# New load order, placement and rank tables in a gated cross-attention and expert kernel

## The chip, the cores and the metric

The kernel runs on one core of a Trainium2 chip. Its time is the device time of one execution in microseconds (us); the median of three runs is compared. TensorE is called PE in the profile, VectorE DVE, ScalarE ACT, GpSimd POOL and SyncE SP.

## The reference

Two token blocks of 1024 rows of 2048 values (x) and two contexts of 2048 by 2048 (ctx) give two gated steps:

```
q1 = fake_quant(layernorm(x), s1, z1)      # round, clip to 0..255, back
q2 = fake_quant(ctx, s2, z2)
x  = x + tanh(g_xattn) * (q1 @ q2)
n  = layernorm(x)
logits = n @ route_w.T                     # 8 experts, the best one is taken
h  = n @ A.T                               # 8 experts x 16
x  = x + tanh(g_ffn) * (onehot(best) * best_logit * h) @ Bw
```

## The kernel before

The 2 x 1024 rows are 16 tiles of 128 rows (eight for each batch); the 2048 output columns are four strips of 512. A tile and a strip make a group: 16 products of 128x128 by 128x512 in float16 (line 718), added up in one PSUM bank. VectorE then adds the result to the tile of x (739, or 747 and 752).

Before that, a tile needs its statistics (bn_stats on VectorE, line 573, for tiles in `STATV`; else a sum and a sum of squares on ScalarE, 591 and 601), an inverse root on GpSimd (623), small scale values on VectorE (613 to 619), quantisation on ScalarE (637), a clamp on VectorE (643), and turning: by eight PE transposes twice (674) and two copies out of PSUM (535, called from 681; the second on VectorE for tiles in `COPYV`), or by one DMA transpose for tiles in `TURN` (664). For tiles in `SPLIT`, VectorE quantises the second half (646, 652). A row sum corrects for the zero points (689 on VectorE for tiles in `SUMV`, 691 on ScalarE).

A context strip comes in four chunks of 1 MB (443), or in two halves each for chunks in `FINE`. A chunk is quantised on ScalarE (450) and clamped on VectorE (457), or, for chunk halves numbered 2 x chunk + half in `VQ`, both on VectorE (461, 468). Its column sums come from 16 PE products with ones (493) for strips in `ONES`, else from VectorE additions and one product (504 to 519).

After a tile's four groups follows the second step: the tile is turned (by PE, 836, and ScalarE copies, 850; or, for tiles in `MOVE`, by VectorE block transposes, 774, and DMA moves, 792, which go by way of DRAM for tiles in `VIA`, 784 and 797, and are issued half on ScalarE's queue for tiles in `TWO`), multiplied with the weights (842 or 818), routed on VectorE (910 to 919), turned back (932, 938), multiplied again (945), added (953) and stored (966 on GpSimd's queue, 959 for the last tile). Tiles in `LATE` add the correction beforehand (730).

All instructions are tasks of a plan. A task has an engine, a cost, a rank, the tasks that it needs and the buffers that it takes. `walk` goes through a model of the engines and, on each engine that is free, picks the ready task of lowest rank that has room; the order found is the order of the program, and on the chip each engine keeps to it. `XL0` and `XLEAD` set the ranks of the loads of x, `CTX` and `CQ` those of context chunks, `LEAD` those of a tile's preparation, `SUM` of its row sum, `COR` of a strip's column sums, `AFTER` and `POR` of the second step and of its output products. `PIECES` cuts a load of x, `XPOOL` puts it on GpSimd's queue; tile 0's second and fourth pieces go by ScalarE's. `SLACK` is added in the model to the landing of loads of x. `XL` loads wait for the last context chunk. At most eight transfers are under way on SyncE's and ScalarE's queues together, and eight on GpSimd's. A DMA transpose is started only when the model's DMA is idle.

The groups run in sets, each set going strip by strip through its tiles:

```
sets = [[0, 1, 2], [3], [4], [5, 6, 7], [8, 9]] + [[t] for t in range(10, NT)]
```

A group's rank is its number in this order, so tiles 0, 1 and 2 share the first strips. The first instructions on PE are warm-up products on a constant (367).

Of the kernel before, what the change touches and what calls it, by code (L numbers as in the profile page):

```python
# [42 lines left out]
class Plan:  # L43
# [11 lines left out]
    def add(self, eng, cost, rank, fn, needs=(), bufs=(), nbytes=0, alone=False, slack=0.0, parts=1):  # L55


        t = Task()
        t.eng, t.cost, t.rank, t.fn, t.nbytes = eng, cost, rank, fn, nbytes
        t.alone, t.slack, t.parts = alone, slack, parts  # L60
        t.needs, t.bufs, t.start, t.end = list(needs), list(bufs), None, None
        for b in bufs:
            b.left += 1
        self.tasks.append(t)
        return t
# [99 lines left out]
def flamingo_gated_kernel(  # L165
# [40 lines left out]
    BLK = 32  # L206


    TURN = {4, 6, 11, 12, 13, 14, 15}
    MOVE = {3, 4, 6, 8, 10, 11, 12, 13, 14}  # L210
    pools = {"big": 10, "q2": 4, "half": 3, "q1t": 5, "wh": 2, "wht": 2, "bn": 3, "sel": 2, "away": 2}
    kinds = {k: (k, n) for k, n in pools.items()}
# [13 lines left out]
    def buf(kind, name, shape, dt):  # L226
        pool = kinds[kind][0]
        where = {"bank": psum, "away": away}.get(pool, work)
        return Buf(kind, lambda u: where.tile(shape, dt, tag=f"{pool}{u}", name=name))
# [68 lines left out]
                whole[t, s] = i  # L298


    LATE = {4, 5, 6, 7, 10, 15}
    STATV = {0, 1, 3, 5, 12, 13, 14}
    SUMV = {2, 5, 6, 8, 12, 14}
    COPYV = {0, 3, 4, 5, 7, 9, 14}
    ONES = {0}
    SUM = [0.5, 8.5, 2.5, 1.5, -1, 1.5, 1.5, 2.5, 5.5, 2.5, 8.5, 1.5, 8.5, 8.5, 1.5, 8.5]
    LEAD = [6, 14, 10, 8, 6, 5, 8, 14, 5, 5, 8, 14, 4, 6, 4, 6]
    XLEAD = [4, 4, 4, 4, 0, 4, 3, 10, 2, 10, 3, 1, 4, 2, 6, 0]
    XL0 = {0: -101, 1: 2.2, 2: -4.0, 3: 4.4}
    AFTER = [1.2, 6.2, 2.2, 2.2, 0.3, -0.8, 4.2, 5.2, -0.8, 3.2, 6.2, 6.2, 4.2, 1.7, 5.2, 2.2]  # L310
    CTX = [8, 6, 5, 5, 5, 5, 4, 3]
    COR = [2.5, 1.5, 7.5, 0.5, 1.5, 1.5, -0.5, 0.5]
    SLACK = 4.0
    VIA = {0, 2, 3, 5, 9, 12, 14}
    TWO = {0, 1, 4, 5, 7, 9, 11, 13, 15}
    XL = {15}
    PIECES = {0: 4, 1: 4, 2: 2, 3: 4}
    SPLIT = {0}
    FINE = {3, 6}
    VQ = {0, 4, 5, 6, 8, 9, 15, 17, 19, 21, 27, 33, 39, 44, 51}  # L320
    XPOOL = {2}
    POR = [0, 0, 1.5, 1, 0, 2, 1.5, 0, 1.5, 0.5, 0, 0.5, 0, 1, 2, 1.5]
    BN2 = set()
    CQ = {4: -1.2, 5: -1.6, 0: 1.2, 11: -1.3, 9: -0.9, 3: 0.6, 7: 0.8, 8: -0.9, 2: 1.3, 6: -2.0, 10: -1.1, 1: 1.3}
    SP, ACT, DVE, PE, POOL = "SP", "ACT", "DVE", "PE", "POOL"
    add = plan.add

# [98 lines left out]
    def strip(b, s):  # L426
# [5 lines left out]
        for q in range(NQ):  # L432
            st = flat(f"st{b}", f"st_{b}_{s}_{q}", F32, D)
            key = (b * NN + s) * NQ + q
            H = 2 if key in FINE else 1
            n = QK // H
            for h in range(H):
                rank = i - CTX[b * NN + s] + (q + h / H) * len(tiles) / NQ + CQ.get(key, 0)
                k = q * QK + h * n
# [31 lines left out]

                on_v = 2 * key + h in VQ
                a = t_ctx[b, s, q] = add(
# [11 lines left out]
        cs = buf("cs", f"cs_{b}_{s}", [P, NC], F32)  # L485
        rank = i + COR[b * NN + s]
        if b * NN + s in ONES:
# [46 lines left out]
    def copy(on_vector, o, i):  # L534
        (nc.vector.tensor_copy if on_vector else nc.scalar.copy)(o, i)  # L535

    def tokens(t):

        b, m = divmod(t, MT)
        early = t == 0  # L540
        rank = first[t] - LEAD[t]
        xb[t] = xx = buf("xl" if t in XL else "x", f"x_{t}", [P, D], F32)
        pieces = PIECES.get(t, 1)
        w = D // pieces
        loads = []
        for i in range(pieces):
            queue = (
                (ACT, nc.scalar) if early and i % 2 else (POOL, nc.gpsimd) if t in XPOOL else (SP, nc.sync)
            )
            loads.append(  # L550
                add(
                    queue[0], 0.5, XL0.get(t, rank - XLEAD[t]),
                    lambda i=i, queue=queue: queue[1].dma_start(
                        xx.ap()[:, ts(i, w)], x[b, ts(m, P), ts(i, w)]
                    ),
                    [t_ctx[1, NN - 1, NQ - 1]] if t in XL else [t_ctx[0, NN - 1, 1]] if t > 3 else [], [xx], nbytes=4 * P * w, slack=SLACK if t > 3 else 0.0 if t else 1.0,
                )
# [9 lines left out]
        mean, var, nmean, ssum = (mv[:, i : i + 1] for i in range(4))  # L567
        if t in STATV:
            bn = buf("bn", f"bn_{t}", [P, NN, 6], F32)
# [41 lines left out]
        def scale():  # L611
# [5 lines left out]
            nc.vector.scalar_tensor_tensor(nb, nmean, a, z1, ALU.mult, ALU.add)  # L617
            if t in SPLIT:
                nc.vector.scalar_tensor_tensor(nv, nmean, a, zm1, ALU.mult, ALU.add)
# [4 lines left out]
        )  # L624
        ts_ = add(DVE, 1.0 if t in SPLIT else 0.8, rank, scale, [pw, t_rs, t_nm])
        if t == 0:
            t_sc.needs.append(ts_)
        q1t[t] = qt = buf("q1t", f"q1t_{t}", [P, KC, P], F16)
        H = 2 if early or t in SPLIT else 1
        hw = D // H  # L630
# [3 lines left out]
        for h in range(H):  # L634
# [18 lines left out]

            on_v = h == 1 and t in SPLIT
            d = add(
# [4 lines left out]
            t_read.setdefault(t, []).append(d)  # L660
        if t in TURN:
            a_ = add(
# [5 lines left out]
            t_turned.append(a_)  # L668
        for h in range(0 if t in TURN else KC // 8):
            pt = buf("tp", f"pq_{t}_{h}", [P, 8, P], F16)  # L670

            def turn(h=h, pt=pt):
                for j in range(8):
# [5 lines left out]
                add(  # L679
                    DVE if h and t in COPYV else ACT, 0.7 if h and t in COPYV else 1.0, rank,  # L680
                    lambda h=h, pt=pt: copy(h and t in COPYV, qt.ap()[:, ts(h, 8), :], pt.ap()),
                    [a_], [pt, qt],
# [3 lines left out]
        def row_sum():  # L686
            p = qb.ap()
            if t in SUMV:
                nc.vector.tensor_scalar(p, p, 0.0, 0.0, ALU.add, ALU.add, accum_out=rw)
# [3 lines left out]
        d = add(  # L693
            DVE if t in SUMV else ACT, 2.3 if t in SUMV else 2.1, first[t] + SUM[t], row_sum, clamps + t_turned, [qb]
        )
        t_r[t] = add(
            DVE, 0.25, first[t] + SUM[t],
            lambda: nc.vector.tensor_scalar(r, rw, cd2, ckd, ALU.mult, ALU.add), [d, t_sc],  # L698
# [7 lines left out]

    late = LATE

# [53 lines left out]
    def hidden_moved(t, xx, hl, rank):  # L762
# [17 lines left out]
        moved = []  # L780
        if t in VIA:
            there = buf("away", f"away_{t}", [P, D], F32)
# [4 lines left out]
        for g in range(BPC):  # L787
            on, queue = (ACT, nc.scalar) if t in TWO and g % 2 else (SP, nc.sync)

# [6 lines left out]
            def fetch(g=g, queue=queue):  # L796
# [6 lines left out]
                add(on, 0.55, rank - 0.5, fetch, [w], [there, across], nbytes=4 * P * NC)  # L803
                if t in VIA
                else add(on, 2.4, rank - 0.5, move, turns, [turned, across], nbytes=4 * P * NC, parts=4)
# [50 lines left out]
    def ffn(t):  # L856
        b, m = divmod(t, MT)
        end = t == NT - 1
        rank = last[t] + AFTER[t]
        xx = xb[t]  # L860
# [65 lines left out]
        a = add(DVE, 1.5, rank - 1, route, [p, t_r2, t_set], [hl, wh, sel_b])  # L926
        behind = rank + POR[t]
        pw = buf("tp", f"pw_{t}", [P, NC], F32)
# [96 lines left out]
```

## Time and profile before

| what | us |
|---|---|
| median of 3 runs | 392.39 (392.09 to 394.58) |
| profiled execution | 393.32 |
| its span | 391.4 |
| TensorE busy | 375.3 |
| VectorE busy | 307.8 |
| ScalarE busy | 228.6 |
| main products, 1024 of line 718, share of the chain of work | 56% |
| output products, 128 of line 945, share of the chain | 14% |

The span is what the trace covers of the profiled execution. The chain of work follows the end of the program back, at each step to what released it, so its shares say which engine the time was spent on. Pipelined products overlap in the busy time: a main product is listed with 379 ns, while they follow each other every 0.216 us. Slices are fortieths of the span. The mean granted clock of TensorE is 0.993.

### The profile page before, as it was taken

The page shows a single profiled execution, that of the slowest core. Times are in us where ns is not written, and L with a number is a line of the kernel's source. Part 1 is how long each engine was busy: PE and PEld are TensorE (multiplying, and loading weights), DVE is VectorE, ACT ScalarE, POOL GpSimd, SP SyncE. Part 2 cuts the span into 40 slices and gives each one's busy share as a digit, 9 for nine tenths or more (in the row PEclk, how much of TensorE's full clock was granted, in tenths as well). Part 3 has the DMA queues.
Part 4 walks back from the last instruction along what each step waited for, and adds up shares of the span by engine and source line. Part 5 has one row for each costly group of instructions (what it writes and reads, how often), then busy time and mean ns, then how long its engine had stood idle before and what let it go on. Part 6 is the DMA issues. An engine that isn't in the chain of part 4 may idle for free.

```text
span 391.4 us, 5431 instructions
## 1 busy us (share of the span) xinstructions
PE 375.3 (96%) x2001; PEld 219.0 (56%) x2001; DVE 307.8 (79%) x709; ACT 228.6 (58%) x219; POOL 22.9 (6%) x54
## 2 busy tenths in 40 slices
PE   5689999999999999999999999999999999999993
PEld 5544545667754464644565754656444664664671
DVE  4599999997786869789888898978989698575243
ACT  1689995489903553887989897556225620430420
POOL 4000000001001000001000010000110000001000
PEclk9899999999999999999999999999999999999998
DMA  7999999601357926989388986348364466509305
GB/s 246 394 386 387 386 351 415 234 0 37 126 215 296 249 60 204 327 316 379 98 207 293 391 353 185 122 137 262 154 127 108 91 225 175 190 42 266 125 1 214
DMA packets 47043, 85.88 MB, mean 219 GB/s; under 512 B 17704, under 2 KB 19752, under 8 KB 43048
## 3 DMA queue, kind: packets, MB, share of 16 engines
q1 hardware_dynamic: 43060, 66.66, 52.3%
q0 software_dynamic: 2512, 16.78, 10.9%
q10 hardware_dynamic: 1444, 2.10, 2.1%
q8 instruction: 15, 0.25, 0.3%
q14 instruction: 12, 0.10, 0.1%
HBM read 55.64 MB, written 19.92 MB: 193 GB/s over the span
## 4 chain that ended last, share of the span: by engine, by line
PE 91%; ACT 3%; DMA 2%; issue 1%; POOL 1%; DVE 0%; POOLq 0%; ACTq 0%
PE mm L718 56%; PE po L945 14%; PE hl L818 9%; PE hl L842 7%; PE px L836 3%; DMA x<-in_x_dram 2%; PE pq L674 2%; ACT q L637 1%; ACT q L450 1%; ACT q L601 1%; ACT q1t L535 1%; ACT q L691 0%; PE pw L932 0%; PE cs L519 0%; POOL row L265 0%
## 5 line engine op out<-in xcount | busy, mean ns | idle before, releaser
L718 PE MATMUL mm<-q,q1t 128*128 128x512 f16 x1024 | 233.3, 379 | 0.7 <-ACT q1t L535 0.7
L718 PEld LDWEIGHTS <-q1t 128*128 128x128 f16 x1024 | 99.8, 98 | 119.1 <-issue 10.9
L450 ACT ACTIVATE q<-st,raw,rs 128x2048 int16<-128x2048 f32 (+1 forms) x29 | 57.6, 2003 | 11.7 <-PE mm L718 8.7
L945 PE MATMUL po<-wb,wht 128*128 128x512 f32 x128 | 60.6, 595 | 0.4 <-ACT wht L938 0.4
L953 DVE SCALAR_TENSOR_TENSOR x<-po,th,x 128x512 f32<-128x512 f32 x64 | 47.1, 748 | 13.2 <-PE po L945 10.7
L637 ACT ACTIVATE q<-x,mine 128x2048 int16<-128x2048 f32 (+1 forms) x16 | 32.6, 2040 | 24.2 <-DVE mine L617 14.8
L899 ACT ACTIVATE junk<-x,mine 128x2048 f16<-128x2048 f32 x16 | 32.1, 2007 | 15.4 <-DVE mine L698 8.0
L818 PEld LDWEIGHTS hl<-war,turned 128*128 128x128 f32 x288 | 34.8, 190 | 2.7 <-issue 1.1
L818 PE MATMUL hl<-war,turned 128*128 128x136 f32 x288 | 35.3, 280 | 0.1
L945 PEld LDWEIGHTS po<-wb,wht 128*128 128x128 f32 x128 | 23.4, 190 | 21.3 <-issue 14.9
L747 DVE SCALAR_TENSOR_TENSOR x<-mm,sc,x 128x512 f32<-128x512 f32 x40 | 29.4, 744 | 4.1 <-PE mm L718 3.7
L752 DVE SCALAR_TENSOR_TENSOR x<-x,mine,corr 128x512 f32<-128x512 f32 x40 | 29.4, 746 | 1.1 <-DVE x L747 0.5
L814 ACT COPY turned<-across 128x1024 f32<-128x1024 f32 x18 | 18.0, 1040 | 20.2 <-DMA across<-away 15.0
L842 PE MATMUL hl<-war,xt 128*128 128x136 f32 x224 | 28.9, 279 | 0.0
L842 PEld LDWEIGHTS hl<-war,xt 128*128 128x128 f32 x224 | 27.9, 190 | 1.6 <-issue 0.5
L739 DVE SCALAR_TENSOR_TENSOR x<-mm,sc,x 128x512 f32<-128x512 f32 x24 | 17.6, 746 | 12.4 <-PE mm L718 12.3
L691 ACT ACTIVATE q<-q 128x2048 f16<-128x2048 f16 x10 | 19.1, 1907 | 9.1 <-DMA q1t<-q 9.1
L774 DVE STREAM_TRANSPOSE turned<-x 128x512 f32<-128x512 f32 x36 | 24.1, 693 | 0.0
L850 ACT COPY xt<-px 128x512 f32<-128x512 f32 x28 | 15.5, 591 | 13.2 <-PE px L836 13.2
L938 ACT COPY wht<-pw 128x128 f32<-128x128 f32 x16 | 4.2, 260 | 30.6 <-PE pw L932 30.6
L457 DVE TENSOR_SCALAR q<-q 128x2048 f16<-128x2048 int16 (+1 forms) x29 | 19.1, 662 | 3.5 <-ACT q L450 3.5
L573 DVE BATCH_NORM_STATS2 bn<-x 128x6 f32<-128x512 f32 x28 | 17.9, 681 | 4.8 <-DMA x<-in_x_dram 4.8
(94 smaller groups left out, 324.7 us busy)
## 6 DMA issues: line engine op xcount, KB each, us to landing
st<-in_ctx_dram SPq DMA_DIRECT2D x30, 1024.0 KB, 9.2
out_dram<-x POOLq DMA_DIRECT2D x15, 1024.0 KB, 5.4
x<-in_x_dram SPq DMA_DIRECT2D x12, 1024.0 KB, 6.1
across<-turned SPq DMA_DIRECT2D x72, 64.0 KB, 2.0
away<-turned SPq DMA_DIRECT2D x3, 1024.0 KB, 6.1
across<-away SPq DMA_DIRECT2D x12, 256.0 KB, 6.3
x<-in_x_dram SPq DMA_DIRECT2D x10, 256.0 KB, 10.4
st<-in_ctx_dram SPq DMA_DIRECT2D x4, 512.0 KB, 11.6
```

What stands on the lines that cost most here:

```text
L450: nc.scalar.activation(part.bitcast(I16), st.ap().rearrange("p (k n) -> p k n", k=QK)[:, ts(h, n)], AF.Relu, bias=z2, scale=rs2,)
L457: nc.vector.tensor_scalar(part, part.bitcast(I16), QMAX, MID, ALU.min, ALU.subtract)
L637: nc.scalar.activation(qb.ap()[:, ts(h, hw)].bitcast(I16), xx.ap()[:, ts(h, hw)], AF.Relu, bias=nb, scale=a)
L718: lambda k=k: nc.tensor.matmul(acc.ap(), qt.ap()[:, k, :], qb.ap()[:, k, :], start=(k == 0), stop=(k == KC - 1)),
L747: lambda: nc.vector.scalar_tensor_tensor(xs(), acc.ap(), c, xs(), ALU.mult, ALU.add),
L752: lambda: nc.vector.scalar_tensor_tensor(xs(), xs(), rs_[t], corr[:, ts(s, NC)], ALU.add, ALU.add, accum_out=ss),
L774: nc.vector.transpose(turned.ap().rearrange("p (g k i) -> p k g i", i=BLK, k=KC)[:, ts(n, BPC)], xx.ap()[:, ts(n, NC)].rearrange("p (k g j ...
L818: nc.tensor.matmul(hl.ap()[:, : ER + E], turned.ap()[:, ts(k, P)], war[:, k, :], start=(k == 0), stop=(k == KC - 1),)
L842: nc.tensor.matmul(hl.ap()[:, : ER + E], xt.ap()[:, ts(k, P)], war[:, k, :], start=(k == 0), stop=(k == KC - 1),)
L899: lambda: nc.scalar.activation(junk.ap(), xx.ap(), AF.Square, bias=nm, accum_out=sq),
L945: lambda n=n, po=po: nc.tensor.matmul(po.ap(), wht.ap(), wb[:, ts(n, NC)], start=True, stop=True),
L953: nc.vector.scalar_tensor_tensor(xs, po.ap(), gf, xs, ALU.mult, ALU.add)
```

## The change

Only tables change. Tile 2's load leaves GpSimd's queue for SyncE's (tile 7's goes the other way); loads of tiles 1 and 2 get ranks among the first context chunks. Tile 2's statistics go to VectorE, tile 13's to ScalarE. Tile 9 is turned by DMA. No tile's quantisation is split between engines any more. The chunks cut in halves and those quantised on VectorE are others, as are the tiles whose row sums, second copies and moves run on one engine, queue or way or another. All ranks are new.

```
-    TURN = {4, 6, 11, 12, 13, 14, 15}
+    TURN = {4, 6, 9, 11, 12, 13, 14, 15}
...
-    LATE = {4, 5, 6, 7, 10, 15}
-    STATV = {0, 1, 3, 5, 12, 13, 14}
-    SUMV = {2, 5, 6, 8, 12, 14}
-    COPYV = {0, 3, 4, 5, 7, 9, 14}
+    LATE = {4, 5, 6, 7, 15}
+    STATV = {0, 1, 2, 3, 5, 12, 14}
+    SUMV = {5, 6, 9, 12, 14}
+    COPYV = {0, 3, 5, 7, 8, 10, 14, 15}
     ONES = {0}
-    SUM = [0.5, 8.5, 2.5, 1.5, -1, 1.5, 1.5, 2.5, 5.5, 2.5, 8.5, 1.5, 8.5, 8.5, 1.5, 8.5]
-    LEAD = [6, 14, 10, 8, 6, 5, 8, 14, 5, 5, 8, 14, 4, 6, 4, 6]
-    XLEAD = [4, 4, 4, 4, 0, 4, 3, 10, 2, 10, 3, 1, 4, 2, 6, 0]
-    XL0 = {0: -101, 1: 2.2, 2: -4.0, 3: 4.4}
-    AFTER = [1.2, 6.2, 2.2, 2.2, 0.3, -0.8, 4.2, 5.2, -0.8, 3.2, 6.2, 6.2, 4.2, 1.7, 5.2, 2.2]
-    CTX = [8, 6, 5, 5, 5, 5, 4, 3]
-    COR = [2.5, 1.5, 7.5, 0.5, 1.5, 1.5, -0.5, 0.5]
-    SLACK = 4.0
-    VIA = {0, 2, 3, 5, 9, 12, 14}
-    TWO = {0, 1, 4, 5, 7, 9, 11, 13, 15}
-    XL = {15}
-    PIECES = {0: 4, 1: 4, 2: 2, 3: 4}
-    SPLIT = {0}
-    FINE = {3, 6}
-    VQ = {0, 4, 5, 6, 8, 9, 15, 17, 19, 21, 27, 33, 39, 44, 51}
-    XPOOL = {2}
-    POR = [0, 0, 1.5, 1, 0, 2, 1.5, 0, 1.5, 0.5, 0, 0.5, 0, 1, 2, 1.5]
+    SUM = [0.5, -1, 2.5, -1, 5.5, 5.5, 2.5, 1.5, 0.5, -1, 8.5, 1.5, 8.5, 1.5, 8.5, 8.5]
+    LEAD = [4, 2, 5, 5, 4, 7, 6, 14, 4, 6, 7, 14, 5, 6, 5, 4]
+    XLEAD = [4, 4, 4, 4, 6, 2, 8, 0, 6, 10, 1, 0, 8, 6, 10, 3]
+    XL0 = {0: -101, 1: -5.6, 2: -3.1, 3: 0.2}
+    AFTER = [1.2, 6.2, 2.2, 0.3, 1.2, -0.8, 0.3, 5.2, 1.2, -0.8, 6.2, 1.2, 2.2, 3.2, 4.2, 1.2]
+    CTX = [5, 4, 5, 5, 5, 5, 5, 5]
+    COR = [7.5, 3.5, 0.5, 1.5, 7.5, 0.5, -0.5, 2.5]
+    SLACK = 2.0
+    VIA = {0, 1, 3, 5, 8, 11, 12, 13}
+    TWO = {0, 3, 4, 7, 12, 13, 14, 15}
+    XL = {13, 15}
+    PIECES = {0: 4, 1: 4, 2: 1, 3: 2}
+    SPLIT = set()
+    FINE = {1, 2, 3, 5, 7}
+    VQ = {3, 5, 8, 9, 14, 15, 19, 33, 39, 44, 45, 51, 62}
+    XPOOL = {7}
+    POR = [3, 0, 0, 2, 3, 3, 4, 2, 1, 0, 4, 0, 6, 2, 0, 3]
...
-    CQ = {4: -1.2, 5: -1.6, 0: 1.2, 11: -1.3, 9: -0.9, 3: 0.6, 7: 0.8, 8: -0.9, 2: 1.3, 6: -2.0, 10: -1.1, 1: 1.3}
+    CQ = {4: -0.1, 5: -0.7, 0: -1.4, 11: -0.1, 9: 0.5, 3: 1.5, 7: 1.0, 8: 1.2, 2: -1.0, 6: -0.6, 10: -0.2, 1: -0.5}
```

## The prediction

> **What bounds the kernel now.** I read the page first (engine shares, the forty slices, the chain), then busy time by stretches, then the timeline of the first 36 us, then the end of the chain in order of time.
>
> ```profile
> span 391.4 us, 5431 instructions
> PE 375.3 (96%) x2001; PEld 219.0 (56%) x2001; DVE 307.8 (79%) x709; ACT 228.6 (58%) x219; POOL 22.9 (6%) x54
> ...
> PE   5689999999999999999999999999999999999993
> ...
> PE 91%; ACT 3%; DMA 2%; issue 1%; POOL 1%; DVE 0%; POOLq 0%; ACTq 0%
> ```
>
> TensorE is 91% of the chain and full in every slice but the first few and the last one. So a change can win only at the two ends or by taking work off TensorE; in between it can only lose. The table by stretches (columns: length, busy us of PE, PEld, DVE, ACT, POOL, granted clock, DMA share, GB/s) puts numbers on it.
>
> ```profile
> 0.00:22.00 22.00, 13.57 (x65) 11.27 (x66) 12.37 (x36) 10.50 (x11) 5.17 (x25) 0.92 0.91 327
> 22.00:28.00 6.00, 5.28 (x37) 2.71 (x36) 5.90 (x14) 6.00 (x6) 0.72 (x1) 1.00 1.04 386
> 28.00:36.00 8.00, 7.99 (x49) 3.95 (x48) 7.33 (x13) 6.98 (x7) 0.00 (x0) 1.00 1.05 386
> 36.00:60.00 24.00, 24.00 (x126) 11.65 (x125) 23.62 (x49) 22.94 (x16) 0.55 (x1) 1.00 1.06 374
> 60.00:80.00 20.00, 20.00 (x109) 11.16 (x108) 18.80 (x27) 11.19 (x12) 0.00 (x1) 1.00 0.74 290
> 80.00:370.00 290.00, 289.90 (x1543) 168.25 (x1542) 231.12 (x552) 167.28 (x164) 15.93 (x26) 1.00 0.61 194
> ```
>
> From 36 to 370 us TensorE stands still for 0.1 us. VectorE is nearly full from 36 to 80 (42.4 of 44 us). The 13.57 us before 22 are mostly warm-up products on a constant. What counts by 27.16 us, at the chain's prices: two tiles turned (16 transposes 0.89 us each, 1.78), twelve column-sum and twelve main products (24 x 0.2157 = 5.18). That is 6.96 us of work, so 20.2 us are lost; after that TensorE hardly waits until the tail. The timeline shows where they went (start, duration, what, idle before it):
>
> ```profile
> 3.97 1.13 POOL L553 DMA_DIRECT2D x<-in_x_dram  x2
> ...
> 9.43 0.22 DVE L617 SCALAR_TENSOR_TENSOR mine<-mine,raw 128x1 f32<-128x1 f32 x1
> ...
> 13.19 1.91 ACT L591 ACTIVATE q<-x 128x2048 f16<-128x2048 f32 x1 [4.83 <-DMA x<-in_x_dram]
> ...
> 15.10 1.23 ACT L637 ACTIVATE q<-x,mine 128x1024 int16<-128x1024 f32 x1
> ...
> 17.75 1.03 PE L674 MATMUL pq<-idh,q 128*128 128x128 f16 x8 [3.67 <-DVE q L643]
> ...
> 27.16 4.49 PE L718 MATMUL mm<-q,q1t 128*128 128x512 f16 x20 [0.72 <-ACT q1t L535]
> ```
>
> ScalarE works in order. Its next instruction after the set-up is tile 2's row sum, for data that GpSimd's queue requested at 3.97 and that landed at 13.1. Behind it stands tile 0's first quantisation, whose scale was ready at 9.65 but which starts at 15.10. VectorE then waits for the same chain (the tiny L596 at 15.22). First main product: 21.94; second tile's 27.16; third tile's 35.8.
>
> **The change, part by part.** Sums are made against the profiled execution: 393.32 us, 1.92 around its span of 391.4. The median shown, 392.39, is 0.93 lower; I apply the difference to that.
>
> *Start: tile 2's statistics, queues, first loads.* Statistics of tile 2 leave ScalarE: 1.91 + 0.19 + 1.99 + 0.18 = 4.3 us and the 4.83 us wait. They become four bn_stats of 0.68 and an aggregate of 0.26 on VectorE, 3.0 us; its row sum (2.28 us, and just in front of a clamp at 30.9) goes to ScalarE (2.1). Tile 0's second half goes from VectorE (0.81 + 0.43 + 0.21) to ScalarE (1.23) with a 0.42 clamp. Chunk quantisation on VectorE goes from four and a half 1 MB chunks to five (about +1.0). By count both engines end within 1 us of where they were, but they start: ScalarE at 9.65 instead of 13.19, VectorE working between 11.8 and 15.2, where it waited.
>
> Loads by the new ranks on SyncE: tile 0, chunk 0, tile 1, halves 1a 2a 1b 2b, tile 2, 3a, 3b. Bytes moved before (140, 356, 402, 386 GB/s per 5 us) reach these sums, 2.1, 3.15, 5.24, 6.29, 7.34 MB, at 8.9, 11.7, 16.9, 19.7, 22.4 us. Landing is later: chunk 0, tile 0 and tile 2 of before (3.15 MB) had landed at 13.1, not 11.7, so I add 1.3: chunk 0 10.2, tile 1 13.0, 2b 18.2, tile 2 21.0, 3b 23.7.
>
> Tile 0: two halves on ScalarE from 9.65, with chunk 0 (2.09) between or behind; all by 14.2. Transposes after the warm-up, which ends at 13.5 (8.01 + 5.49), then a copy (1.0): first main product near 15.5. Tile 1: landing 13.0, last bn_stats 0.7, then 2.3 to the scale (26.71 to 29.0 in the trace), quantisation 2.09 behind half chunks, then 2.5 for clamp, turn and copy: 21.5. Tile 2: 21.0 + 0.7 + 2.3 + 2.09 + 1.5 of queueing + 2.5 = 30. So all three tiles come about 6 us earlier. By 30 us TensorE has done three turns 2.67, sixteen column sums 3.45, 32 products 6.90, and some of the second strip's first chunk 0.9: 13.9, lost 16.1 instead of 20.4 at 35.8. Gain 4.3; I take **-4.2**. Best bound: nothing lost after 15.5 except that less 0.89 of turns, 14.6, so -5.8. Worst: a late tile 1 or 2 holds VectorE as it held ScalarE (4.83), +0.6. I stay nearer the first, since bn_stats wait for pieces that come one by one, with little else yet to do. Past 30 us DMA still runs at 386 GB/s, one chunk in 2.7 us against 3 x 0.86 = 2.6 of products, so TensorE can just be fed.
>
> The number of cut chunks grows from two to five. The trace moves 385 to 388 GB/s with 256 KB, 512 KB and 1 MB loads in flight together, so I cost that at 0.
> The Trainium skill, DMA: Bandwidth & Descriptors, section Bandwidth, advises at least 1 MiB per DMA for 75% of peak. By its fit (2.0 us fixed per DMA) three more cuts would be an estimated 6 us of extra DMA time and the start would gain nothing; the rate here speaks against it with several loads in flight.
>
> *Tile 9 turned by DMA.* Sixteen transposes leave TensorE: **-0.9**; copies of 1.0 and 0.68 go too. The DMA transpose lands in 4.4 us. Cover: tile 9's rank is six groups ahead of its first group, 6 x 3.45 = 20.7 us. Without cover it costs up to a chunk landing, 9.2 us.
>
> *The rest.* Tile 13's statistics to ScalarE (4.3) off VectorE (3.3); tile 10 no longer late (VectorE 5.7 to 6.3); row sums on VectorE six to five; DRAM detours three to five tiles, each 6.1 + 6.3 us of landing against sixteen issues of 2.0; 22 instead of 24 such issues on ScalarE. Tile 13's load now waits for the last context chunk, and tile 7's goes to GpSimd's queue, where it stands among the outputs (GpSimd waits up to 25.3 us for these). After 80 us VectorE (231 of 290) and ScalarE (167) hide their parts. Loads are planned with 2 us of slack instead of 4. Nothing can be gained there; **0**, with up to 9.2 lost.
>
> *Tail.* By the ranks the output products of tile 14 come at 59 + 4.2 = 63.2, ahead of tile 15's hidden products (64.2); before they came behind them (66.2 against 65.2) and covered tile 15's routing. The end of the chain in order of time (start, length, what):
>
> ```profile
> 373.47 3.71 PE hl L842 x32
> 377.38 0.28 ACT wht L938
> 377.70 1.98 PE po L945 x4
> 379.79 5.17 PE po L945 x12
> 384.98 0.75 DVE x L953
> ```
>
> Uncovered, routing (1.3), turn and copy cost 2.2 instead of 0.5: +1.7. But tile 14's 1 MB output, issued at 382.59 among the last four stores, goes earlier; they land in 4.6 us now, a lone small one in 2.0 to 3: about -1.4. Together **+0.3**, bounds -1.5 and +1.7.
>
> Sum: -4.2 - 0.9 + 0 + 0.3 = -4.8; profiled 388.5, median **387.6 us**.
>
> **Rivals.** (A) VectorE becomes the bound. From 36 to 80 us it has 1.6 us idle, and it evacuates every product. If what it gains is only the wait at 11.8 to 15.2 less the 1 us of added quantisation, the start is worth 2.4 and the whole -3.0: 389.4; if its low-rank work cannot slip, 391. For: 98% busy at 36 to 60. Against: row sums and column sums there can wait until after 120, where it is 20% idle.
> (B) Slower: tile 9's transpose. It is issued only when the plan sees the DMA idle, and DMA is 78% busy from 160 to 200 (the turn by TensorE was at 187.8). If it lands a chunk (9.2 us) after its first group is due, TensorE, in order, stands: 387.6 + 9.2 = 396.8. It turns the result slower once it is more than 8.7 us late, since 4.8 are in hand and 1% is 3.9. For: SyncE's queue once stood 31.5 us at such a transpose. Against: 20.7 us of lead.
> (C) The start doesn't do what it says: VectorE waits for late tile 1 or 2 and holds back tile 0's clamps: +0.6 in place of -4.2, 392.4.
>
> **How the numbers follow.** Forecast 0.50, A 0.25, B 0.15, C 0.10 (the rule on small DMAs is within C, 0.02). A measurement of this kernel can tell about 1%, 3.9 us, from no change. Faster than 388.5: 0.42 of the forecast's 0.50 and 0.06 of A, 0.48. Slower than 396.3: 0.10 of B and 0.07 for a similar late landing elsewhere, taken from the others: 0.17. Same: 0.35. The forecast's own range is 385 to 389.5; with A, C and part of B the range is 384.5 to 396.
>
> **What would show it.** ScalarE's first tile-0 quantisation starts near 10 us, not 15.1; first main product 15 to 17; TensorE loss at 36 us near 16; pq 128 transposes instead of 144; eight DMA transposes; no stop of TensorE above 0.5 us between 36 and 368; an idle of about 2 us in front of tile 15's output products. Wrong if VectorE sits on a load in the first 20 us, if PE idles before 60 us on VectorE, or if a wait for q1t stands at tiles 8 and 9.

## The result, and the profile after

The changed kernel takes 391.86 us (median of 22 runs, 391.27 to 394.02) against 393.53 for the kernel before (22 runs on the same chip): a ratio of 0.9948, interval 0.9928 to 0.9968. So it is faster by about 2 us, within the 1% that was called the same, and well short of the 4.8 us forecast. The profiled execution took 391.43 us with a span of 389.7 (before 393.32 and 391.4).

From the page of the changed kernel: the span, the busy times, TensorE's forty slices and the shares of the chain of work.

```profile
span 389.7 us, 5389 instructions
...
PE 372.4 (96%) x1985; PEld 216.2 (55%) x1985; DVE 307.9 (79%) x714; ACT 230.4 (59%) x220; POOL 23.6 (6%) x53
...
PE   5699999899999999999999999999999999999994
...
PE 78%; DMA 14%; ACT 4%; SPq 1%; issue 1%; DVE 1%; ACTq 0%
```

Sixteen products fewer on TensorE (1985 for 2001), as the change says. Two things differ from before: a digit 8 in the eighth slice (68 to 78 us), and a DMA share of 14% in the chain, where it was 2%. A transfer has got into the path. The table by stretches finds it (length, busy us of PE, PEld, DVE, ACT, POOL, granted clock, DMA share, GB/s):

```profile
0.00:22.00 22.00, 14.43 (x82) 11.06 (x83) 15.20 (x45) 13.31 (x12) 4.10 (x23) 1.00 0.90 321
22.00:28.00 6.00, 5.78 (x38) 2.73 (x36) 4.23 (x14) 5.61 (x5) 0.55 (x1) 1.00 1.04 393
28.00:36.00 8.00, 7.36 (x47) 3.60 (x45) 7.96 (x16) 7.60 (x9) 0.00 (x0) 1.00 1.05 388
36.00:60.00 24.00, 24.00 (x130) 12.03 (x128) 22.69 (x41) 22.25 (x15) 1.17 (x2) 1.00 1.07 380
60.00:80.00 20.00, 18.12 (x102) 10.55 (x100) 17.18 (x30) 12.68 (x15) 0.00 (x0) 1.00 0.63 236
80.00:370.00 290.00, 289.26 (x1529) 167.28 (x1528) 232.02 (x551) 166.13 (x160) 17.27 (x26) 1.00 0.65 207
```

From 60 to 80 us TensorE now stands 1.88 us (before 0.00), and after 80 it stands 0.74 (before 0.10).

A matmul that waits between two others is listed as busy, so the comparison uses TensorE's loss, as the prediction did: the time less the work done by then, counted by matmuls at the chain's prices (main products and column sums 0.2157 us, a transpose of q 0.0557, of x 0.109, a product with the weights 0.116, an output product 0.4295). In us, from the profiled executions:

| loss by | before | after | difference |
|---|---|---|---|
| 36 us | 20.38 | 17.58 | -2.80 |
| 68 us | 20.42 | 17.82 | -2.60 |
| 76 us | 20.41 | 20.07 | -0.34 |
| 266 us | 21.49 | 20.01 | -1.48 |
| 270 us | 21.56 | 21.19 | -0.37 |
| 366 us | 21.57 | 21.17 | -0.40 |

So the start won 2.8 us; 2.3 of them went between 68 and 76 us. What was won again by 266 (the kernel before loses 0.4 between 90 and 200 us and 0.8 between 200 and 240) went in a second stop at 268. With tile 9's transposes gone (0.9) the last main product ends 1.26 us earlier, at 366.75 instead of 368.01. From there to the end of the output products takes 18.61 us instead of 16.97 (+1.64), and from there to the end of the span 4.34 instead of 6.42 (-2.08). The sum is -1.26 + 1.64 - 2.08 = -1.70, the difference of the spans.

**The start.** ScalarE's timeline (start, length, what, and in brackets the idle before it with its releaser):

```profile
9.71 2.09 ACT L450 ACTIVATE q<-st,raw,rs 128x2048 int16<-128x2048 f32 x1 [0.69 <-DMA st<-in_ctx_dram]
11.71 2.36 ACT L637 ACTIVATE q<-x,mine 128x1024 int16<-128x1024 f32 x2
14.52 2.59 ACT L450 ACTIVATE q<-st,raw,rs 128x1024 int16<-128x1024 f32 x2 [0.46 <-DMA st<-in_ctx_dram]
17.02 0.99 ACT L535 COPY q1t<-pq 128x1024 f16<-128x1024 f16 x1
17.91 2.09 ACT L637 ACTIVATE q<-x,mine 128x2048 int16<-128x2048 f32 x1
...
22.39 1.01 ACT L535 COPY q1t<-pq 128x1024 f16<-128x1024 f16 x1 [0.50 <-PE pq L674]
```

The 4.83 us wait for tile 2 is gone, and tile 0 is quantised at 11.71, right behind the first chunk, instead of 15.10. But tile 0's first copy (L535) stands behind two half chunks until 17.02, though its transposes were done at 14.70; the first main product starts at 18.07. Tile 1's first copy ends at 23.40.

**The stop at 69 us.** Lines of SyncE's queue, ScalarE and TensorE from one timeline:

```profile
49.32 0.50 SPq L384 DMA_DIRECT2D war<-in_w_ar_dram  x1
49.87 7.20 SPq L387 DMA_DIRECT2D wb<-in_w_b_dram  x1
57.16 0.38 SPq L443 DMA_DIRECT2D st<-in_ctx_dram  x1
...
68.59 2.09 ACT L450 ACTIVATE q<-st,raw,rs 128x2048 int16<-128x2048 f32 x1 [3.96 <-DMA st<-in_ctx_dram]
...
71.46 2.75 PE L718 MATMUL mm<-q,q1t 128*128 128x512 f16 x12 [1.88 <-DVE q L457]
```

The last context chunk of the first batch is issued behind the loads of the second step's weights (384 and 387). The second of these issues stands for 7.20 us on SyncE. The chunk lands at 68.6, ScalarE has waited 3.96 us for it and TensorE 1.88. Before, it landed at 66.05, when TensorE was 2.6 us further behind and did not yet need it (ScalarE, kernel before):

```profile
66.05 2.10 ACT L450 ACTIVATE q<-st,raw,rs 128x2048 int16<-128x2048 f32 x1 [0.50 <-DMA st<-in_ctx_dram]
```

The kernel before had its long issue too (8.62 us behind the same load of 384, from 45.90), and TensorE did not stand. There, too, both loads of weights went ahead of this chunk, and by 66 us both kernels had moved 24.0 MB. What is new ahead of the chunk is another load: tile 7's, now on GpSimd's queue, which lands 7.9 us after its issue, at about 62 (changed kernel: GpSimd's timeline, and the same issue in the list of DMAs with its time to landing):

```profile
54.24 0.62 POOL L553 DMA_DIRECT2D x<-in_x_dram  x1 [16.40 <-ACT q L450]
...
x<-in_x_dram POOLq DMA_DIRECT2D x1, 1024.0 KB, 7.9
```

Its 1 MB takes some 2.6 us at the 400 GB/s moved from 58 to 60 us, and the chunk is 2.5 us later. This is read from the traces; no run moves tile 7's load alone.

**The stop at 268 us** (ScalarE, then TensorE):

```profile
268.58 1.99 ACT L814 COPY turned<-across 128x1024 f32<-128x1024 f32 x2 [3.66 <-DMA across<-away]
...
269.68 3.97 PE L818 MATMUL hl<-war,turned 128*128 128x136 f32 x32 [0.74 <-ACT turned L814]
```

Tile 8 now goes by way of DRAM (it is new in `VIA`), and its second fetch lands late.

**The tail.** From the chain in order of time (start, length, what):

```profile
378.53 0.94 PE hl L842 x8
...
380.91 0.31 PE pw L932
...
381.31 0.27 ACT wht L938
...
381.62 3.71 PE po L945 x8
...
385.36 0.75 DVE x L953
```

Between 379.47 and 381.62 TensorE does nothing but one small product of the routing: 2.15 us uncovered, where before output products of tile 14 lay.

### The profile page after: what moved, and what is told of

The parts are those of the page before. It is cut to its first block, busy times and chain, and to the rows that moved or that the text cites. A ratio compares the mean times of both kernels' runs of the same rounds, so it can differ in the third digit from the quotient of the medians.

```text
span 389.7 us, 5389 instructions
## 1 busy us (share of the span) xinstructions
PE 372.4 (96%) x1985; PEld 216.2 (55%) x1985; DVE 307.9 (79%) x714; ACT 230.4 (59%) x220; POOL 23.6 (6%) x53
## 4 chain that ended last, share of the span: by engine, by line
PE 78%; DMA 14%; ACT 4%; SPq 1%; issue 1%; DVE 1%; ACTq 0%
PE mm L718 45%; PE po L945 13%; DMA st<-in_ctx_dram 11%; PE hl L818 9%; PE hl L842 7%; PE px L836 2%; DMA across<-away 2%; ACT q L450 2%; DMA x<-in_x_dram 1%; PE pq L674 1%; ACT q1t L535 1%; ACT q L637 1%; ACT q L691 0%; PE pw L932 0%; PE cs L493 0%
## 5 line engine op out<-in xcount | busy, mean ns | idle before, releaser
L637 ACT ACTIVATE q<-x,mine 128x2048 int16<-128x2048 f32 (+1 forms) x17 | 33.7, 1990 | 14.4 <-DVE mine L617 13.3
L752 DVE SCALAR_TENSOR_TENSOR x<-x,mine,corr 128x512 f32<-128x512 f32 x44 | 32.0, 747 | 0.7 <-ACT corr L526 0.2
L691 ACT ACTIVATE q<-q 128x2048 f16<-128x2048 f16 x11 | 21.0, 1906 | 5.8 <-DVE turned L774 5.8
```

The source lines that it names most:

```text
L637: nc.scalar.activation(qb.ap()[:, ts(h, hw)].bitcast(I16), xx.ap()[:, ts(h, hw)], AF.Relu, bias=nb, scale=a)
L691: nc.scalar.activation(p, p, AF.Copy, accum_out=rw)
L752: lambda: nc.vector.scalar_tensor_tensor(xs(), xs(), rs_[t], corr[:, ts(s, NC)], ALU.add, ALU.add, accum_out=ss),
```

## The experiments

All are made from the changed kernel. Where an instruction is moved, it is moved in the finished order, so that nothing else changes its place:

```
     order = plan.walk()
+    def after(task, other):
+        order.remove(task)
+        order.insert(order.index(other) + 1, task)
```

Ratios are to the kernel before, with their intervals. Theory: the forecast's gain was there, and three waits took it; first of all the chunk at 68 us, whose cover was the time that TensorE had been behind. Rivals: that VectorE is the bound anyway, or that the start is what fell short. f1, f2 and f3 change tables, so their whole order is planned anew.

**1. e1, the wide vector load behind the last chunk** (`after(t_wb, t_ctx[0, NN - 1, NQ - 1])`: line 387 behind the last issue of 443).

> The changed kernel with one move in the order on SyncE's queue: the load of wb (1 MB) goes behind the last context chunk of the first batch instead of in front of it; nothing else moves. Theory: TensorE's 2.3 us stop at 68.6 to 71.5 is that chunk (landed 68.6), held back by 1 MB of wb in the same queue, 2.7 us at 386 GB/s. Then the chunk lands near 66, the stop is gone, TensorE's loss at 76 us goes from 20.1 to about 17.8, and the kernel takes some 2.2 us less than the changed one (span near 387.4). Rival: the chunk is late because the queue's issue stood still behind the load of war (7.2 us); then it lands at 68 as before, and the time stays (span 389.6).

Measured: 389.70 us (389.04 to 391.44, 6 runs), 0.9909 (0.9885 to 0.9934), 2.2 us below the changed kernel (the kernel before beside it took 393.54, as beside the changed one). The chunk's issue now comes first on SyncE's queue:

```profile
53.43 3.76 SPq L443 DMA_DIRECT2D st<-in_ctx_dram  x1
57.24 0.81 SPq L387 DMA_DIRECT2D wb<-in_w_b_dram  x1
```

TensorE's products run through, without idle, where it stood 1.88 us. The rival was the long issue itself. It is out: the long issue is still there, now the chunk's own, and ends at 57.19 where the chunk's issue ended at 57.54 in the changed kernel; yet ScalarE starts on the chunk at 66.59 without waiting. In e6, below, the same issue stands for 5.82 us and ends at 56.90, and the chunk lands at 65.86. What had held the chunk back was the megabyte of wb ahead of it. Taking tile 7's megabyte out of its way should do the same; only wb's was tried.

The profiled execution itself had a worse start (first chunk landed at 12.0, granted clock 0.50 from 16 to 22 us, loss at 36 of 19.95) and lost nothing from there to 76 (20.07). That this is the 20.07 of the changed kernel is chance. That a late start and a late chunk do not add up is shown by the execution of e4 (experiment 5), which leaves SyncE's order as it is in the changed kernel and had both (ScalarE):

```profile
69.15 2.09 ACT L450 ACTIVATE q<-st,raw,rs 128x2048 int16<-128x2048 f32 x1 [2.07 <-DMA st<-in_ctx_dram]
```

Its loss at 36 us was 20.17 and at 76 20.66, half a microsecond more, where the changed kernel loses 2.5 in this stretch.

**2. e7, the same chunk later still** (`after(t_ctx[0, NN - 1, NQ - 1], t_x[4][0])`: behind tile 4's load).

> The changed kernel with the last context chunk of the first batch put one load further back, behind tile 4's 1 MB. Theory (its landing sets where TensorE is at 76 us, whatever the start does): it lands 2.7 us later, near 71.3; loss at 76 us rises from 20.1 to 22.5 to 22.8 in every run, and the kernel takes 2.5 us more than the changed one (span 392.2), slower starts or not. Rival (the stop at 68 is an accident of one run): no change, span 389.6.

Measured: 395.61 us (394.54 to 398.25), 1.0032 (1.0009 to 1.0055), 3.7 above the changed kernel, 3.3 by the ratios (the kernel before took 394.13 beside it). From one timeline, and below it a stretch of the table:

```profile
71.03 2.10 ACT L450 ACTIVATE q<-st,raw,rs 128x2048 int16<-128x2048 f32 x1 [6.37 <-DMA st<-in_ctx_dram]
...
73.91 4.42 PE L718 MATMUL mm<-q,q1t 128*128 128x512 f16 x10 [4.29 <-DVE q L457]
```

```profile
72.00:76.00 4.00, 2.09 (x6) 0.70 (x6) 2.81 (x3) 4.00 (x5) 0.00 (x0) 0.60 0.44 103
76.00:80.00 4.00, 4.00 (x15) 2.23 (x14) 2.15 (x6) 1.51 (x3) 0.00 (x0) 0.55 0.43 163
```

The chunk lands 2.44 us later and TensorE idles 2.41 longer: one for one, so the path goes through this chunk. The loss at 80 is 25.12, 5 above the changed kernel's: 2.4 are the idle, and most of the rest comes with the granted clock, which fell to 0.60 and 0.55 behind an idle of 4.29 us and did not behind 1.88.

**3. e3 and e5, tile 0's copies ahead** of the half chunks (e3 alone, e5 together with e1's edit):

```
+    after(turns_of[0][0], clamps_of[0][0])
+    after(t_q1t[0][0], turns_of[0][0])
+    after(t_q1t[0][1], t_scale[1])
```

> The changed kernel with tile 0's two copies out of PSUM moved ahead: the first in front of the half chunks 1a and 2a on ScalarE, the second in front of the two half chunks quantised on VectorE. Theory one (the copies stand in the queue, as the prediction had not seen): first main product near 16 instead of 18.1, and the start's loss falls by about 2 us for good (loss at 36 us 15.6 instead of 17.6). Theory two (the start is bound by the data of strip 0 and the next chunk): the first product comes earlier, but TensorE stands again before 30 us, where the second strip's first chunk lands at 27.6; loss at 36 us stays 17.4 to 17.7 and the span 389.6.

> The move of wb behind the last context chunk together with tile 0's copies out of PSUM moved ahead. Theory (the start was masked by the late chunk, and is itself bound by data near 28 to 30 us): as the run with wb alone, lowest time near 389.0, median 389.7; loss at 76 us that of its own start, 17.5 to 20, with the chunk's stop gone. Rival (the copies' place is worth 2 us once the mask is off): lowest time near 387.

Measured: e3 392.23 us (390.82 to 393.47), 0.9966 (0.9948 to 0.9984); e5 391.68 (389.68 to 393.19), 0.9927 (0.9898 to 0.9956). Neither gained. In e5 the first product came at 17.53, but the clock fell, in e3 likewise (first product 18.16, loss at 36 of 19.09). The table of e5 from 16 to 20 us:

```profile
16.00:18.00 2.00, 2.00 (x12) 0.84 (x10) 0.39 (x2) 2.00 (x3) 0.56 (x1) 0.62 1.09 413
18.00:20.00 2.00, 2.00 (x6) 0.69 (x5) 1.89 (x9) 1.70 (x2) 0.00 (x0) 0.53 0.99 406
```

So the copies could be without worth, or the clock could have taken it. That was settled last:

**4. h0 to h3, order, clock or data.** h0 is the best kernel of these runs (its edits are under 5 and 6). h1 adds to it e3's move, and tile 1's scale values (613 to 617) ahead of the clamp that waits for a half chunk; h3 adds six idle products on a constant behind tile 0's transposes, to keep the clock; h2 has h1's order and three idle products.

> The kernel with all three later edits (wide vector load behind the last chunk, tail covered, tile 8's sorts ahead of tile 15's row sum) once more, as the base of the three below on the same chip. Expected: TensorE's loss at 36 us 17.1 to 18.0, the same at 76, first main product 18.1 to 18.5, median 388.1 within 0.6.

> The base, with tile 0's two copies moved ahead of the half chunks 1a and 2a, and tile 1's scale values ahead of the clamp that waits for half chunk 1a on VectorE; nothing else moves. Theory 1, the order of the two queues holds the start: first main product at 16.1 to 16.5, tile 1's quantisation no later than 18.6, loss at 36 us lower by 0.8 to 1.4, median lower by as much. Theory 2, the clock: it falls to 0.5 between 16 and 20 us as in the two runs with early copies, and the loss stays within 0.4 of the base. Theory 3, the data: the products that can start early are four, the rest wait for half chunks that land at 14 and later, clock 1.0, and the loss falls by under 0.4.

> The order of the run before, and three idle products on a constant (6 passes, 0.7 us) behind tile 0's turn, so that TensorE's idle there is short. Theory 1: as the run before, loss 0.8 to 1.4 below the base. Theory 2: now the clock stays at 1.0 and the loss falls by 0.8 to 1.4, in this run alone. Theory 3: within 0.4 of the base.

> The base order, and six idle products on a constant (12 passes, 1.3 us) behind tile 0's turn, in front of the first column sums, in the idle that ends with the first copy. Theory 2: the clock never falls in the first 24 us, the median is as the fastest of the base and the spread narrower. Theories 1 and 3: loss at 36 within 0.3 of the base, median within 0.4.

Measured: h0 388.01 us, h1 388.24, h2 387.84, h3 388.05, with ratios of 0.9845 (0.9814 to 0.9875), 0.9849 (0.9819 to 0.9879), 0.9841 (0.9811 to 0.9872) and 0.9862 (0.9821 to 0.9903): all alike. The granted clock was 1.00 from 8 to 24 us in all four, so the clock is out of it here. TensorE in h1:

```profile
15.99 1.03 PE L718 MATMUL mm<-q,q1t 128*128 128x512 f16 x4
17.34 0.59 PE L718 MATMUL mm<-q,q1t 128*128 128x512 f16 x2 [0.33 <-DVE q L457]
19.37 0.59 PE L718 MATMUL mm<-q,q1t 128*128 128x512 f16 x2 [1.44 <-DVE q L468]
...
23.46 4.81 PE L718 MATMUL mm<-q,q1t 128*128 128x512 f16 x21 [0.23 <-ACT q1t L535]
```

The first product is 2.1 us earlier (h0: 18.10), and TensorE gives it all back waiting for a half chunk on VectorE (L468). Tile 1's products start at 23.46, in h0 at 23.49, and the loss at 36 is 17.58 in both. The third theory holds: the first product is not what the start is measured by, for tile 0 alone has 0.86 us of products per chunk. What holds, by these lines, is tile 1. On VectorE in h1:

```profile
18.05 0.81 DVE L461 TENSOR_SCALAR q<-st,rs,zm 128x1024 int16<-128x1024 f32 x1
18.89 0.43 DVE L468 TENSOR_SCALAR q<-q 128x1024 f16<-128x1024 int16 x1
19.24 0.81 DVE L461 TENSOR_SCALAR q<-st,rs,zm 128x1024 int16<-128x1024 f32 x1
20.08 0.43 DVE L468 TENSOR_SCALAR q<-q 128x1024 f16<-128x1024 int16 x1
20.42 0.69 DVE L643 TENSOR_SCALAR q<-q 128x2048 f16<-128x2048 int16 x1
```

ScalarE had quantised tile 1 by 19.57 in h1 (0.37 earlier than in h0), but its clamp (L643) stands behind two half chunks that VectorE quantises, at 20.42 as in the changed kernel (20.45). Moving that clamp was not tried; by these lines it is worth at most 0.85 us.

**5. e4 and e6, the tail covered again.** Two of tile 14's four output groups go behind tile 15's last product with the weights, where TensorE waits for the routing (e4 alone, e6 with e1's edit):

```
+    after(po14[2], hl15)
+    after(po14[3], po14[2])
+    after(fin14[2], route15)
+    after(fin14[3], fin14[2])
+    after(store14, fin14[3])
```

> The changed kernel with the last two of tile 14's output products put behind tile 15's last hidden product, their additions behind tile 15's routing, and the store of tile 14 behind these. Theory: TensorE's end comes 1.7 us earlier (its wait of 2.15 us in front of tile 15's output products falls to about 0.4), but the 1 MB store of tile 14 now runs with the last four stores, so the stretch from the last product to the end of the span grows from 4.3 to about 6: span changes by -0.5 to +0.5 us. Rival: the stores don't matter, and the span falls by 1.7.

> The move of wb together with the rearranged end (last two of tile 14's output products behind tile 15's last hidden product). Theory: the sum of both alone, -2.2 and -0.3 against the changed kernel: lowest near 388.7, median near 389.4. Rival: nothing beyond the run with wb alone, 389.0 and 389.7.

Measured: e4 391.33 us (390.92 to 391.60), 0.9940 (0.9917 to 0.9963). The output products end 16.95 us after the last main product instead of 18.61, but the span ends 5.68 after them instead of 4.34: of the 1.66 won, 1.34 goes back into tile 14's later store. e6: 389.05 (388.62 to 389.64, 6 runs), 0.9869 (0.9844 to 0.9895), TensorE's loss at 76 of 17.64. So the chunk's stop and the tail are separate, and the start's gain of 2.8 comes through to the end.

**6. The stop at 268 us: e2, g6, f3.** In e2 tile 15's load goes behind tile 8's fetches (with e1's edit). In g6 this is added to e6, and tile 8's two copies (814) go ahead of tile 15's row sum (591) on ScalarE. In f3 tile 9 is turned by TensorE again, with e1's edit.

```
+    after(t_x[15][0], fetch_of[8][-1])
+    for sort in sort_of[8]:                      # g6 only
+        order.remove(sort)
+        order.insert(order.index(sum_of[15]), sort)
...
-    TURN = {4, 6, 9, 11, 12, 13, 14, 15}         # f3 only
+    TURN = {4, 6, 11, 12, 13, 14, 15}
```

> As the run with wb behind the chunk, and tile 15's load (1 MB) behind tile 8's four fetches from DRAM on SyncE's queue, instead of between its write to DRAM and these fetches. Theory: TensorE's 1.1 us stop at 268 to 270 is those fetches, landing 2.7 us late behind 1 MB: another 1.1 us less than the first run, so 3.3 less than the changed kernel (span near 386.3), loss at 300 us 17.8 or so instead of 21.1. Rival: the stop comes back later, because tile 15's data or the next DMA transpose is late: span as in the first run.

> Wide vector load behind the last context chunk and the covered tail (the fastest pair so far), and for the stop at 268 us: tile 15's load behind tile 8's fetches on SyncE's queue, and tile 8's two sorts ahead of tile 15's row sum on ScalarE. Theory: of the two waits that took turns there, both are now off ScalarE's path, so TensorE's loss grows by under 0.2 us from 266 to 270 (1.1 before the edit), and the time is 1.0 below that pair's 389.05: 388.0. Rival: the sorts still wait for fetches that DRAM moves hold up; then the stop stays at about 1.1 and the time within 0.5 of 389.

> As the run with wb moved, with tile 9 turned by TensorE and two copies again instead of by DMA (the plan of the order changes with it, after tile 9's preparation). Theory: TensorE has 16 transposes, 0.89 us, more, with no stop saved: +0.9 against the run with wb alone (lowest 389.9). Rival A: the stop of 1.0 us at 268 to 270 comes from a DMA transpose between the fetches and goes with it, so the time stays. Rival B: TensorE's 0.9 fills a wait that is there anyway, and the time stays too, with the loss 0.9 lower at the end.

Measured: e2 390.96 us (389.51 to 394.41), 0.9936 (0.9909 to 0.9963), no better than e1. The fetch was no longer late, but ScalarE stood at tile 15's row sum, with tile 8's copies behind it:

```profile
265.77 1.91 ACT L591 ACTIVATE q<-x 128x2048 f16<-128x2048 f32 x1 [6.16 <-DMA x<-in_x_dram]
267.58 0.19 ACT L591 ACTIVATION_READ_ACCUMULATOR q<-x 128x1 f32 x1
267.68 1.98 ACT L814 COPY turned<-across 128x1024 f32<-128x1024 f32 x2
```

The loss from 266 to 270 grew by 1.97 (18.29 to 20.26): a wait undone let the next one in line take its place, larger. With both out of the way g6 has copies first:

```profile
263.04 1.99 ACT L814 COPY turned<-across 128x1024 f32<-128x1024 f32 x2 [3.64 <-DMA across<-away]
265.37 1.91 ACT L591 ACTIVATE q<-x 128x2048 f16<-128x2048 f32 x1 [0.33 <-DMA x<-in_x_dram]
```

Its loss from 266 to 270 is 0 (18.07, 18.06), and its time 388.13 (387.72 to 390.68, 6 runs), 0.9891 (0.9864 to 0.9918); run once more, as h0, 388.01, 0.9845 (0.9814 to 0.9875). In us that is 0.9 below e6, where 1.0 was expected; the ratios of e6 and g6, from different chips, overlap (and g6 and h0, the same kernel, differ by 0.5% in theirs), so the gain rests on the loss in the traces. f3: 391.81 (390.98 to 395.98), 0.9953 (0.9928 to 0.9977). Its loss does not grow at 268, but by 1.2 from 300 to 340 us, and it pays the 0.9 of transposes: in these two plans tile 9's DMA transpose is worth having, and it is only one of several transfers that meet here.

**7. f1 and f2, the two halves of the start.** Both are e6 with one part of the change undone, and both plans are made anew, so only the first 36 us are compared. f1 gives tile 2's statistics back to ScalarE (`STATV` without 2), f2 tile 2's load to GpSimd's queue (`XPOOL = {2, 7}`).

> The fastest pair (wide vector load behind the last chunk, covered tail) with tile 2's statistics back on ScalarE, its load left on SyncE's queue; the plan is made anew, so orders past 60 us differ and the start alone is compared: TensorE's loss at 36 us, 17.2 to 18 with the statistics on VectorE. In the plan tile 2's sum now stands behind tile 0's row sum, not ahead of tile 0's quantisation. Theory (ScalarE's place in line, not its work, cost the kernel before its start): tile 0's first quantisation stays at 11.7 and the first product at 18; the 4.3 us of sums push tile 1's copies back by about 4, and the loss at 36 becomes 19 to 20.5. Rival (statistics are only work that fits anywhere): loss at 36 within 0.5 of 17.6.

> The fastest pair with tile 2's load back on GpSimd's queue at the head of the program, its statistics left on VectorE; the plan is made anew, tile 2 takes tile 1's place in the order and tile 0's quantisation goes ahead of the first chunk. The start alone is compared. Theory (the queue was not what held the start back, the in-order wait of ScalarE was): tile 0's first quantisation at about 10, first product at 16.5 to 18, loss at 36 of 16.5 to 18.5. Rival (the early megabyte takes the DMA's rate from tile 0 and chunk 0): first quantisation at 11 or later, first product after 18.5, loss at 36 over 19.

Measured: loss at 36 us 23.22 in f1 and 20.17 in f2, against 17.15 in e6; whole times 396.92 (1.0111, 1.0087 to 1.0135) and 394.85 (1.0051, 1.0031 to 1.0071). ScalarE in f1:

```profile
22.18 1.90 ACT L591 ACTIVATE q<-x 128x2048 f16<-128x2048 f32 x1
...
25.20 1.99 ACT L601 ACTIVATE q<-x,mine 128x2048 f16<-128x2048 f32 x1
...
27.19 1.90 ACT L535 COPY q1t<-pq 128x1024 f16<-128x1024 f16 x2
```

The first product stays (18.44), and tile 1's copies come at 27.19 instead of 22.39, by the 4.3 us of the two sums and a little more; TensorE then stands 1.99 and 1.83 us, and its clock falls to 0.50 to 0.60 from 26 to 32 us, so the loss is above the 20.5 expected. In f2 the rival was right:

```profile
10.00 2.37 ACT L637 ACTIVATE q<-x,mine 128x1024 int16<-128x1024 f32 x2 [1.34 <-DVE mine L617]
...
17.64 2.58 ACT L450 ACTIVATE q<-st,raw,rs 128x1024 int16<-128x1024 f32 x2 [2.18 <-DMA st<-in_ctx_dram]
```

Tile 0 is quantised at 10.00, as my forecast had it, but the half chunks land 3.1 us later (17.64 for 14.52), and the first product starts at 18.57. The granted clock was 0.55 and 0.60 from 16 to 20 us in this execution, so not all of the 3 us of loss need be the queue's. As far as two newly made plans can show it, both parts of the change make the start, each through what lies in line behind it; the queue's part I had thought nothing of.

**8. g5, idle products in the tail.** The changed kernel's times lie from 391.3 to 394.0, and in e5, e7 and f3 the last eight output products took 5.41 us instead of 3.71, at a granted clock of about 0.68. Eight products on a constant fill the idle in front of them (`warm_up(8, 66.5, [tail_of[15][0]])`).

> The changed kernel, with eight idle products on a constant (16 passes, about 1.8 us) put on TensorE in the idle of 2.15 us in front of tile 15's output products; nothing else moves. Theory: the spread of the changed kernel (spans near 389.7 and again near 391.3) and the eight last output products that took 3.71 us in some runs and 5.41 in others are one thing, the clock that falls after that idle. Then the last eight take 3.71 us, the last windows show a granted clock of 1.0, the spread is under 0.6 us, and the median is that of the lower group, 391.0 to 391.6. Rival 1: the idle products come late and push the output products back, up to +1.5. Rival 2: the spread has another source (the start); then it stays 2 us wide.

Measured: 391.72 us, 0.9968 (0.9946 to 0.9989); ten of 12 runs from 391.0 to 392.2, two above (393.83 and 402.83). The last eight took 3.71 us, as they did in the changed kernel's own profile, and the spread is not narrower in any way that 12 runs can show. The theory is not borne out. Of the kernels with the covered tail, e4, e6, f2 and h0 to h2 lie within about 1 us each, f1 within 1.8, and g6 and h3 with one run of six outside; why, stays open.

## Why the prediction was wrong, point by point

The forecast was 387.6 us with 385 to 389.5 as its own range, and 391.86 was measured. Of the 4.3 us between them 1.1 is the kernel before, whose median over 22 runs is 393.53 and not 392.39. The other 3.1 are a gain of 1.7 where 4.8 was forecast.

**The start, -4.2: right in kind, -2.8 in size.** The wait at tile 2's row sum went, as said. The step that failed is the arrival of tile 1, "landing 13.0, last bn_stats 0.7, then 2.3 to the scale ..., quantisation 2.09 behind half chunks, then 2.5 ...: 21.5". Its last bn_stats began at 13.94; the quantisation began at 17.91 behind two half chunks and a copy; its clamp stood on VectorE behind two more half chunks and a copy until 20.45, and its turn on TensorE behind column sums until 21.75. Tile 1 was there at 23.46 instead of 21.5, and tile 2's turn came at 30.64 instead of products at 30. I had added durations of one chain and let two engines that work in order be free for it. (The count "four and a half 1 MB chunks to five" on VectorE is that of the whole kernel; by 36 us VectorE quantised three and a half before and two after, so it was the order of VectorE's work and not its amount that held tile 1.) "First main product near 15.5" failed too (18.07), but h1, at 15.99, shows that this was worth nothing.

**"Past 30 us ... TensorE can just be fed" and the middle's 0: the step that decided.** Between 36 and 76 us it cost +2.46 us, with a stop of 1.88, where no stop above 0.5 was expected. I had read "from 36 to 370 us TensorE stands still for 0.1 us" as slack on the side of the loads. It was the reverse: a kernel that is 2.8 us late finds its last chunk just there. The trace of before had the chunk (landing 66.05, ScalarE waiting 0.50 for it) and I did not ask what a TensorE 2.8 to 4.2 us ahead would find at 66 us. Nor did I ask what tile 7's load, named under "the rest" and put at nothing, would move ahead of: by the traces it is the megabyte that made the chunk 2.5 us later than before. That the chunk's landing did it is shown by e1 (-2.2) and e7 (idle +2.41 for a landing 2.44 later).

**Slower by a late landing (rival B):** right in kind, wrong in place and price. Tile 9's transpose was never late. Tile 8's fetch from DRAM was, and cost 1.1 us; the kernel before lost 1.16 between 76 and 366 us in its own way, so this part came out even (-0.06).

**Tile 9, -0.9:** 0.86 (1.26 earlier less 0.40 of loss); eight DMA transposes and 128 transposes on TensorE, as said.

**The tail, +0.3:** +1.64 where +1.7 was said, and -2.08 where -1.4 was. Together -0.4; e4 shows that the two belong to one store and trade against each other.

**Chunks cut in halves, 0:** no cost is seen. With five chunks in halves the DMA moved 393 and 388 GB/s from 22 to 36 us, before 386 and 386; no run undoes the cuts alone. The rule on small DMAs (the Trainium skill, DMA: Bandwidth & Descriptors, section Bandwidth), with 2.0 us fixed per DMA, would have made the start gain nothing. The Trainium skill gives these 2.0 us (same page, section Anatomy of one DMA) for DMAs issued from GpSimd, and the chunks go by SyncE's queue; with several loads in flight this trace doesn't show such a cost.

**VectorE (rival A)** did not become the bound after 36 us (22.69 of 24 us busy from 36 to 60, less than before), but its order in the first 21 us is what tile 1 waited for.

The sum, in spans: 1.4 less at the start, 2.46 at the chunk, and 0.7 more than forecast from the tail, which leaves the span 3.1 us above the forecast.

## What to carry to other kernels

A gain at the start of a kernel lasts only up to the first transfer that was just in time for the slower one: for each us won, look up which loads land within that margin of their use, further on, and move other loads, on whichever queue, out of their way. When a chain of steps is added up over engines that work in order, add what stands in line ahead of each step, not only its duration. And when a wait is undone, look who stands next behind it: at 268 us the second cost more than the first.

## What the runs showed of the hardware that I had not expected

An issue on SyncE's queue is not always 0.4 us: the one right behind the load of line 384 (1,088 KB in rows of 544 bytes) stood for 8.62 us in the kernel before, 7.20 in the changed one, 3.76 in e1 and 5.82 in e6, whatever it was that it loaded. Another issue, at 22.50 in the changed kernel, stood for 4.07 us, so the short rows are not shown to be the reason. Nor is such an issue by itself a loss: in e1 and e6 the chunk whose issue stood landed 2 us or more earlier than in the changed kernel. Its place among the loads decided that, and by the traces a load on GpSimd's queue counts in that line too.

The granted clock differs between executions of the same order of work: at the start it was 1.00 throughout in the changed kernel, and 0.50 from 16 to 22 us in e1, whose order is the same up to 49 us but whose first chunk landed 2.4 us later (12.0 for 9.6). The same 2.15 us in front of the last eight output products, in which TensorE did nothing but one small product, were followed by a clock that fell to 0.50 to 0.53 in e5, e7 and f3 (5.41 us for 3.71) and by the full clock in the changed kernel and e1; after 4.29 us in e7 it fell too. The Trainium skill, TensorE: Matmul & The Clock Gate, Part 1, explains a spread from run to run by an activity window of about 3.4 us that runs freely, so that it matters where in it the work falls. The runs agree with such a spread, though none shows the window itself. The table there in the Trainium skill puts the fall of the clock behind at least one idle window; here it fell behind 2.15 us, and the measurement decides.
